# Layer 3, second half: normalising the output rows on ScalarE instead of VectorE

## The chip, the cores and the metric

The kernel runs on one core of one Trainium2 chip. The metric is device time in microseconds (us) for one execution of the whole program. The core's engines named here are PE (TensorE, matrix multiply), DVE (VectorE), ACT (ScalarE), POOL (GpSimd) and SP (SyncE, used here only to issue DMA transfers).

## The reference

Four graph-attention layers run one after the other over 3327 nodes of 256 features, all with the same adjacency matrix. Each is followed by a residual sum and a normalisation of every row. Only the last layer matters here; its cut form is:

```python
def _layernorm(x, axis=-1, eps=1e-5):
    m = jnp.mean(x, axis=axis, keepdims=True)
    v = jnp.var(x, axis=axis, keepdims=True)
    return (x - m) / jnp.sqrt(v + eps)

# layer 3: four heads of 64 features, two such passes one after the other
h = jnp.einsum('nf,hfd->hnd', x, W)
e = jax.nn.leaky_relu(f1[:, :, None] + f2[:, None, :], ALPHA)
e = jnp.where(adj[None, :, :] > 0, e, NEG)
att = jax.nn.softmax(e, axis=-1)
out = jax.nn.elu(jnp.einsum('hnm,hmd->hnd', att, h))

x = _layernorm(x + layer3(x, adj))      # the result
```

The change touches only the last line for layer 3: the last step of the normalisation, (x - mean) times 1/sqrt(var + eps), row by row.

## The kernel before

The nodes lie in 26 tiles of 128 rows (the last has 127). The tiles of the result are taken in four blocks of 7, 7, 6 and 6 tiles. The second pass of layer 3 is `many_heads(l3b, None, finish_last)`. For each block it loops over all 26 source tiles j:

- `adjacent` has SP load the adjacency tile `at` for (j, block) from DRAM (line 135 by way of `copy_rows`). There are three buffers for `at`, so SP issues the load of a step when DVE has finished with the tile of three steps earlier.
- `weigh` (line 1629) has DVE make four edge tiles `e`, one for each head, 128 x 896 elements in the blocks of seven and 128 x 768 (767) in the blocks of six. There are eight buffers for `e`, which is two steps of j.
- PE multiplies: line 1773 for the features and line 1781 for the row sums, both fp32. Within a step PE takes the first half of the block's columns for all four heads first, so it needs all four `e` tiles early in its step.

After a block's 26 steps its accumulators are copied out by ACT (lines 1800 and 1802), and `finish_last` for this block is put into the list `pending`. It is a generator: `work_off` takes one piece of it (up to a `yield`) in each step j of the **next** block. So the finishing of blocks 0, 1 and 2 runs among the steps of blocks 1, 2 and 3, and that of block 3 runs alone at the end. DVE, ACT and PE keep the order in which these pieces are emitted here; each engine works its instructions off in that order.

`finish_last` transposes the tiles back on PE (line 1923), scales and applies the elu on ACT and DVE (lines 1930 to 1950), takes the row statistics on DVE (lines 1952 and 1953) into `mv` (mean and variance of each tile), and then calls `scaled`:

```python
            nc.vector.tensor_scalar(rstd, mv[:, :, 1], EPS, None, op0=ALU.add)        # 250, DVE
            nc.gpsimd.tensor_tensor(rstd, rstd, minus_half..., op=ALU.pow)             # 251, POOL
            yield
            for s, it in enumerate(block):
                nc.vector.tensor_scalar(                                               # 257, DVE
                    h[it][:pn], ys[s][:pn], mv[:pn, s, 0:1], rstd[:pn, s : s + 1],
                    op0=ALU.subtract, op1=ALU.mult,
                )
                if s == len(block) // 2:
                    yield
            yield
```

In a block of seven, four tiles are normalised in one step of the loop and three in the following one. The finished tiles `h` are then written to `out_dram` by SP (line 135 again), one DMA for each tile. In SP's queue these writes stand among the loads of `at`.

Of the kernel before, what the change touches and what calls it, by code (L numbers as in the profile page):

```python
# [8 lines left out]
F32 = mybir.dt.float32  # L9
# [4 lines left out]
AF = mybir.ActivationFunctionType  # L14
ALU = mybir.AluOpType
# [4 lines left out]
P = 128  # L20
BANK = 512
SLOPE = 0.2
EPS = 1e-5
# [27 lines left out]
def gat_stack(  # L51
# [29 lines left out]
    nc = tc.nc  # L81
# [7 lines left out]
    def rows_of(it):  # L89
        return min(P, n - it * P)  # L90
# [4 lines left out]
    small = ctx.enter_context(tc.tile_pool(name="small", bufs=4))  # L95
# [4 lines left out]
    minus_half = const.tile([P, 1], F32, name="minus_half")  # L100
# [3 lines left out]
    h = [nodes.tile([P, dim], F32, name=f"h{it}") for it in range(nt)]  # L104
# [24 lines left out]
    def copy_rows(engine, dst, src):  # L129

        rows = dst.shape[0]
        whole = rows // 16 * 16
        for lo, hi in ((0, whole), (whole, rows)):
            if lo < hi:
                engine.dma_start(dst[lo:hi], src[lo:hi])
# [91 lines left out]
    blocks = [list(range(f, f + s)) for f, s in zip(firsts, sizes)]  # L227
# [20 lines left out]
    def scaled(block, ys, mv):  # L248
        rstd = small.tile([P, len(block)], F32, tag="rstds", name="rstds")
        nc.vector.tensor_scalar(rstd, mv[:, :, 1], EPS, None, op0=ALU.add)  # L250
        nc.gpsimd.tensor_tensor(  # L251
            rstd, rstd, minus_half.to_broadcast([P, len(block)]), op=ALU.pow
        )
        yield
        for s, it in enumerate(block):
            pn = rows_of(it)
            nc.vector.tensor_scalar(  # L257
# [6 lines that stand above are left out]
# [1242 lines left out]
    def layers(rs, early=0, rest=None):  # L1506
# [18 lines left out]
        def misc(banks):  # L1525
            spare[0] += 1
            i = banks[spare[0] % len(banks)]
            return ps.tile([P, BANK], F32, tag=f"b{i}", name="misc")
# [276 lines left out]
        def staged(units, stages):  # L1805

            last = max(at for _, at in units) + max(lag for lag, _ in stages)
            for step in range(last + 1):
                for lag, what in reversed(stages):
                    for unit, at in units:  # L1810
                        if at + lag == step:
                            what(unit)
                yield

        def inverses(block, sums, inv):

            full = [s for s, it in enumerate(block) if rows_of(it) == P]
            turned = misc((6, 7))
            for s, it in enumerate(block):
                pn = rows_of(it)  # L1820
                x, at0 = divmod(s, (len(block) + 1) // 2)
                nc.tensor.matmul(  # L1822
                    turned[:pn, s * heads : (s + 1) * heads],
                    sums[x][:, at0 * P : at0 * P + pn], heads_at, start=True, stop=True,
                )
            yield
            w = len(full) * heads
            nc.vector.reciprocal(inv[:, :w], turned[:, :w])
            if len(full) < len(block):
                pn = rows_of(block[-1])  # L1830
                nc.vector.reciprocal(inv[:pn, w : w + heads], turned[:pn, w : w + heads])
            yield
# [3 lines left out]
        def below(dst, v):  # L1836

            nc.scalar.activation(dst, v, AF.Relu, scale=-1.0)
            nc.scalar.activation(dst, dst, AF.Exp, scale=-1.0)
# [69 lines left out]
        def finish_last(b, o, sums):  # L1909
            block = blocks[b]  # L1910
            inv = small.tile([P, max(sizes) * heads], F32, tag="invs", name="invs", bufs=2)
            yield from inverses(block, sums, inv)
            mv = small.tile([P, len(block), 2], F32, tag="mvs", name="mvs")
            if rows_of(block[-1]) < P:
                nc.vector.memset(mv, 1.0)
            held = {}

            def back(s):
                it = block[s]
                pn = rows_of(it)  # L1920
                tp = misc((6, 7))
                for k in range(kc):
                    nc.tensor.transpose(
                        tp[:pn, k * P : (k + 1) * P], o[:, k, s * P : s * P + pn], ident
                    )
                both = work.tile([P, 2, 2 * P], F32, tag="spread", name="both", bufs=4)
                v, t = held[s] = both[:, 0, :], both[:, 1, :]
                if b < len(blocks) - 1:
                    for k in range(heads):
                        nc.scalar.activation(  # L1930
                            v[:pn, k * hd : (k + 1) * hd], tp[:pn, k * hd : (k + 1) * hd], AF.Copy,
                            scale=inv[:pn, s * heads + k : s * heads + k + 1],
                        )
                else:
                    nc.vector.tensor_tensor(
                        v[:pn].rearrange("p (h d) -> p h d", h=heads),
                        tp[:pn, :dim].rearrange("p (h d) -> p h d", h=heads),
                        inv[:pn, s * heads : (s + 1) * heads, None].to_broadcast([pn, heads, hd]),
                        op=ALU.mult,
                    )  # L1940
                below(t[:pn], v[:pn])

            def add(s):
                it = block[s]
                pn = rows_of(it)
                v, t = held.pop(s)
                nc.vector.scalar_tensor_tensor(  # L1947
                    v[:pn], t[:pn], -1.0, v[:pn], op0=ALU.add, op1=ALU.max
                )
                nc.vector.tensor_add(h[it][:pn], v[:pn], h[it][:pn])  # L1950
                stats = small.tile([P, nc.vector.BN_STATS_DIM], F32, tag="stats", name="stats")
                nc.vector.bn_stats(stats[:pn], h[it][:pn])  # L1952
                nc.vector.bn_aggr(mv[:pn, s, :], stats[:pn])

            yield from staged([(s, s) for s in range(len(block))], [(0, back), (3, add)])
            yield from scaled(block, [h[it] for it in block], mv)
            for it in block:
                pn = rows_of(it)
                copy_rows(nc.sync, out[it * P : it * P + pn, :], h[it][:pn])
            yield  # L1960
# [94 lines left out]
        l3b = Layer("l3b", "g", heads, True, load_heads(l3_w2, l3_a2), rate_d=rate3_d[1])  # L2055
        many_heads(l3a, l3b, finish_hidden)
        many_heads(l3b, None, finish_last)
        work_until(lambda: not pending)

# [80 lines left out]
```

## Time and profile before

| what | value |
|---|---|
| median of 3 runs | 2950.82 us (2949.16 to 2955.55) |
| the profiled execution, whole | 2953.03 us |
| its span, first to last instruction | 2951.3 us |
| mean granted TensorE clock over the span | 0.866 |
| PE busy in the span | 2329.5 us (79%) |
| DVE busy in the span | 2140.5 us (73%) |
| ACT busy in the span | 840.2 us (28%) |

All durations come from the one profiled execution, whose time is 1.7 us more than its span and 2.2 us above the median. The profile's times are counted from the start of the span. The second pass of layer 3 begins at about 2443 us. Its blocks 1, 2 and 3, among which `finish_last` runs, end their loops at about 2696, 2810 and 2922 us; the rest, to 2951, is the finishing of block 3. Shares over the whole span say little about this change: only about the last 360 us of the 2951 hold any of it.

### The profile page before, as it was taken

The page shows a single profiled execution, that of the slowest core. Times are in us where ns is not written, and L with a number is a line of the kernel's source. Part 1 is how long each engine was busy: PE and PEld are TensorE (multiplying, and loading weights), DVE is VectorE, ACT ScalarE, POOL GpSimd, SP SyncE. Part 2 cuts the span into 40 slices and gives each one's busy share as a digit, 9 for nine tenths or more (in the row PEclk, how much of TensorE's full clock was granted, in tenths as well). Part 3 has the DMA queues.
Part 4 walks back from the last instruction along what each step waited for, and adds up shares of the span by engine and source line. Part 5 has one row for each costly group of instructions (what it writes and reads, how often), then busy time and mean ns, then how long its engine had stood idle before and what let it go on. Part 6 is the DMA issues. An engine that isn't in the chain of part 4 may idle for free.

```text
span 2951.3 us, 45054 instructions
## 1 busy us (share of the span) xinstructions
PE 2329.5 (79%) x15841; PEld 1364.5 (46%) x15862; DVE 2140.5 (73%) x5634; ACT 840.2 (28%) x2358; POOL 991.6 (34%) x1061
## 2 busy tenths in 40 slices
PE   7466657556545416657899999999999999999997
PEld 4222323222222103325788888863556667534332
DVE  6789789968776527765445521138999999899997
ACT  3244445434334304543344311111010110110111
POOL 2676767777777777771000000000000000000000
PEclk8576777767776656889999999999999999999998
DMA  7685656445644444645776633331222222212211
GB/s 236 198 259 147 189 167 168 141 131 158 166 111 114 111 108 124 173 120 180 221 206 201 187 86 109 107 95 45 77 60 83 74 79 65 70 45 59 59 44 48
DMA packets 183854, 370.50 MB, mean 126 GB/s; under 512 B 35772, under 2 KB 124707, under 8 KB 182596
## 3 DMA queue, kind: packets, MB, share of 16 engines
q1 hardware_dynamic: 103994, 178.49, 21.2%
q0 software_dynamic: 51008, 155.70, 19.1%
q10 hardware_dynamic: 28618, 33.33, 3.3%
q8 instruction: 128, 2.10, 0.3%
q14 instruction: 106, 0.87, 0.1%
HBM read 327.52 MB, written 46.23 MB: 127 GB/s over the span
## 4 chain that ended last, share of the span: by engine, by line
PE 46%; DVE 5%; DMA 2%; issue 1%; ACT 0%; DVEq 0%; SPq 0%; ACTq 0%; POOL 0%; POOLq 0%
PE acc L1773 18%; PE acc L1723 16%; PE acc L1781 9%; DVE e L1629 3%; PE misc L1557 3%; DMA at<-at_d 1%; PE misc L1666 0%; DMA at_d<-at 0%; DMA at_i<-in_adj_t_dram 0%; DVE stats L1952 0%; DVE h L1950 0%; DVE h L1745 0%; DVE both L1947 0%; PE misc L1822 0%; DVE h L257 0%
## 5 line engine op out<-in xcount | busy, mean ns | idle before, releaser
L912 POOL DMA_INDIRECT g<-table_d,lst x894 | 850.8, 952 | 273.1 <-issue 243.4
L1629 DVE SCALAR_TENSOR_TENSOR e<-rate,feat,at 128x896 f32<-128x896 f32 (+4 forms) x832 | 843.4, 1080 | 58.6 <-PE acc L1781 47.2
L1015 PE MATMUL acc<-g,ident 128*128 128x512 f32 (+1 forms) x896 | 516.4, 721 | 257.3 <-ACT g L1012 232.5
L1773 PE MATMUL acc<-e,feat 128*32 128x384 f32 (+2 forms) x6656 | 697.4, 515 | 7.2 <-DVE h L1745 4.2
L1773 PEld LDWEIGHTS acc<-e,feat 128*32 128x32 f32 x6656 | 307.1, 110 | 305.3 <-issue 159.1
L1015 PEld LDWEIGHTS acc<-g,ident 128*128 128x128 f32 x896 | 199.2, 232 | 479.6 <-ACT g L1012 357.2
L1781 PE MATMUL acc<-e,feat 128*32 128x384 f32 (+3 forms) x3328 | 383.3, 512 | 0.0
L1012 ACT ACTIVATE g<-g,w 128x256 f32<-128x256 f32 x883 | 365.5, 495 | 0.4 <-ACT minus L489 0.4
L932 DVE TENSOR_TENSOR y<-g,minus_ps 128x1028 f32<-128x1028 f32 (+2 forms) x233 | 273.3, 1173 | 123.4 <-DMA g<-table_d,lst 113.6
L938 DVE SCALAR_TENSOR_TENSOR y<-y,a_ps 128x257 f32<-128x257 f32 x894 | 324.4, 418 | 26.5 <-PE a_ps L781 6.1
L1723 PE MATMUL acc<-feat,e 128*128 128x257 f32 (+2 forms) x1352 | 303.9, 382 | 7.4 <-DVE inv L1744 4.9
L251 POOL TENSOR_TENSOR rstds<-rstds,minus_half 128x7 f32<-128x7 f32 (+1 forms) x12 | 19.7, 1641 | 773.7 <-DVE rstds L250 773.7
L1723 PEld LDWEIGHTS acc<-feat,e 128*128 128x128 f32 (+2 forms) x1352 | 255.2, 191 | 45.3 <-issue 7.8
L1723 PE MATMUL acc<-feat,at 128*128 128x257 bf16 (+2 forms) x2028 | 237.8, 274 | 4.6 <-DMA at<-at_d 4.4
L1781 PEld LDWEIGHTS acc<-e,feat 128*32 128x32 f32 (+1 forms) x3328 | 162.1, 110 | 130.7 <-issue 88.1
L1723 PEld LDWEIGHTS <-at 128*128 128x128 bf16 (+2 forms) x2028 | 198.8, 99 | 38.3 <-DMA at<-at_d 4.9
L553 PE MATMUL v<-code,leads 65*128 65x512 bf16 (+1 forms) x182 | 83.3, 459 | 155.0 <-DVE cand L579 124.2
L1629 DVE SCALAR_TENSOR_TENSOR e<-rate,feat,at_i 128x896 f32<-128x896 f32 (+2 forms) x104 | 112.3, 1081 | 91.5 <-DMA at_i<-in_adj_t_dram 47.0
L579 DVE MAX8 cand<-v 128x8 f32<-128x104 f32 (+2 forms) x858 | 158.9, 260 | 21.6 <-PE v L556 21.3
L1609 POOL DMA_DIRECT2D rate3b_d<-rate_rows x4 | 2.1, 519 | 450.0 <-ACT rate_rows L1608 450.0
L1656 ACT CAST at<-at_i 128x896 bf16<-128x896 int32 (+2 forms) x104 | 92.0, 885 | 111.5 <-DMA at_i<-in_adj_t_dram 74.8
L553 PEld LDWEIGHTS <-leads 65*128 65x128 bf16 x182 | 22.3, 123 | 189.7 <-DVE cand L579 155.2
(248 smaller groups left out, 1829.3 us busy)
## 6 DMA issues: line engine op xcount, KB each, us to landing
adj_i<-in_adj_dram SPq DMA_DIRECT2D x75, 512.0 KB
at<-at_d SPq DMA_DIRECT2D x150, 224.0 KB
at_i<-in_adj_t_dram SPq DMA_DIRECT2D x50, 448.0 KB
at<-at_d SPq DMA_DIRECT2D x75, 192.0 KB
at<-at_d SPq DMA_DIRECT2D x75, 191.8 KB
g<-table_d,lst POOLq DMA_INDIRECT x894, 2.8
at_d<-at ACTq DMA_DIRECT2D x50, 224.0 KB
at_i<-in_adj_t_dram SPq DMA_DIRECT2D x25, 384.0 KB
```

The lines of the kernel that those rows point to most:

```text
L553: nc.tensor.matmul(v[:, :w], leads[:, b, :], code[:, :w], start=True, stop=False)
L579: nc.vector.max(spread[:, c0 + c, :], view(v[:, :w]))
L912: nc.gpsimd.indirect_dma_start(out=g[:, k - k0, :], out_offset=None, in_=table_d[:, :], in_offset=bass.IndirectOffsetOnAxis(ap=entry["lst" ...
L932: nc.vector.tensor_tensor(y, rows, minus_src[:, None, :].to_broadcast([P, m, dim + 1]), op=ALU.max)
L938: nc.vector.scalar_tensor_tensor(y, y, 1.0, a_ps[:, : dim + 1], op0=ALU.mult, op1=ALU.mult, accum_out=sc)
L1012: nc.scalar.activation(rows, rows, AF.Copy, scale=w[:, k : k + 1])
L1015: nc.tensor.matmul(dst, ident, rows, start=start, stop=stop)
L1629: nc.vector.scalar_tensor_tensor(e[:pn, : c1 - c0], self.rate[b][:pn, h_of, : c1 - c0], q, at[:pn, : c1 - c0], op0=ALU.max, op1=ALU.mult,)
L1656: nc.scalar.copy(at[:pn, :w], at_i[:pn, :w])
L1723: nc.tensor.matmul(accs[s][:pn, : dim + 1], a[:pj, s * P : s * P + pn], f[:pj, : dim + 1], start=(j == 0 and part == 0), stop=(j == nt - 1 ...
L1773: nc.tensor.matmul(accs[x][p][q : q + 32, : hi - lo], f[:pj, at0 : at0 + 32], es[at0 // hd][:pj, lo:hi], start=(j == 0), stop=(j == nt - 1),)
L1781: nc.tensor.matmul(accs[x][pairs][h_of * 32 : (h_of + 1) * 32, : hi - lo], f[:pj, dim + h_of : dim + h_of + 1].to_broadcast([pj, 32]), es[ ...
```

## The change

`finish_last` no longer calls `scaled`. It makes the same `rstd` (DVE add, POOL power), then one further small DVE instruction makes `shift` = -mean * rstd for all tiles of the block. The tiles are then normalised by ACT as `h * rstd + shift`, both taken as one value for each row. In the last block every second tile (s = 1, 3, 5) is still normalised by DVE with the old instruction. The places of the `yield`s stay.

```diff
-            yield from scaled(block, [h[it] for it in block], mv)
+            rstd = small.tile([P, len(block)], F32, tag="rstds", name="rstds")
+            shift = small.tile([P, len(block)], F32, tag="rstds", name="shifts")
+            nc.vector.tensor_scalar(rstd, mv[:, :, 1], EPS, None, op0=ALU.add)
+            nc.gpsimd.tensor_tensor(
+                rstd, rstd, minus_half.to_broadcast([P, len(block)]), op=ALU.pow
+            )
+            yield
+            nc.vector.scalar_tensor_tensor(
+                shift, mv[:, :, 0], -1.0, rstd, op0=ALU.mult, op1=ALU.mult
+            )
+            for s, it in enumerate(block):
+                pn = rows_of(it)
+                if b == len(blocks) - 1 and s % 2:
+                    nc.vector.tensor_scalar(
+                        h[it][:pn], h[it][:pn], mv[:pn, s, 0:1], rstd[:pn, s : s + 1],
+                        op0=ALU.subtract, op1=ALU.mult,
+                    )
+                else:
+                    nc.scalar.activation(
+                        h[it][:pn], h[it][:pn], AF.Identity,
+                        bias=shift[:pn, s : s + 1], scale=rstd[:pn, s : s + 1],
+                    )
+                if s == len(block) // 2:
+                    yield
+            yield
             for it in block:
                 pn = rows_of(it)
                 copy_rows(nc.sync, out[it * P : it * P + pn, :], h[it][:pn])
```

The instruction orders of the two kernels, engine by engine, differ in these places only:

- DVE loses 20 instructions of line 257 in blocks 0, 1 and 2 (7, 7 and 6) and 3 of 6 in block 3; it gains one `shift` in each block, in the place where the first of line 257 stood.
- ACT gains 7, 7, 6 and 3 activations, behind the last elu activation of the same block and ahead of the next block's copies of line 1800.
- SP had, in blocks 0 to 2, four writes of `out_dram`, one load of `at`, and the other two or three writes. Now all six or seven writes stand together behind the twentieth (in the last such place the nineteenth) load of the block, and the load that stood between them comes after. In block 3 the first two writes are exchanged: tile 94 before tile 93.
- PE and POOL keep their order.

## Prediction

> **What bounds the kernel now.** I read three things in this order: the chain of work that ended last, the busy time of the engines in two neighbouring stretches, and the timelines of DVE and PE where the removed instructions stand.
>
> The chain, on the page, says who sets the time over the whole span:
>
> ```profile
> span 2951.3 us, 45054 instructions
> ...
> PE 46%; DVE 5%; DMA 2%; issue 1%; ACT 0%; DVEq 0%; SPq 0%; ACTq 0%; POOL 0%; POOLq 0%
> ```
>
> PE leads, DVE is a small second. The question is whether the DVE part holds the removed instructions. The busy time in two stretches of block 2 of the second pass (the columns are stretch, length, busy time and number for PE, weight loads, DVE, ACT and POOL, then clock, DMA share, GB/s):
>
> ```profile
> 2730.00:2784.00 54.00, 53.28 (x562) 19.41 (x566) 53.28 (x81) 10.57 (x36) 2.11 (x1) 1.00 0.20 58
> 2784.00:2843.00 59.00, 59.00 (x719) 24.24 (x712) 55.83 (x62) 4.64 (x12) 0.00 (x0) 1.00 0.19 52
> ```
>
> PE looks full in both. But it ends 719 matmuls in 59 us (12.2 per us) in the second stretch and 562 in 54 us (10.4 per us) in the first, at the same clock of 1.00. In the first PE is waiting inside its own records, and DVE is the engine without a gap. `finish_last` of block 1 runs in the first stretch only. ACT is busy a fifth of it. The timeline of DVE there (start, duration, line, tiles, number):
>
> ```profile
> 2765.92 3.79 DVE L1629 SCALAR_TENSOR_TENSOR e<-rate,feat,at 128x768 f32<-128x768 f32 x4
> 2769.63 0.16 DVE L250 TENSOR_SCALAR rstds<-mvs 128x7 f32<-128x7 f32 x1
> 2769.70 3.80 DVE L1629 SCALAR_TENSOR_TENSOR e<-rate,feat,at 128x768 f32<-128x768 f32 x4
> 2773.42 1.38 DVE L257 TENSOR_SCALAR h<-h,mvs,rstds 128x256 f32<-128x256 f32 x4
> 2774.71 3.80 DVE L1629 SCALAR_TENSOR_TENSOR e<-rate,feat,at 128x768 f32<-128x768 f32 x4
> 2778.43 1.05 DVE L257 TENSOR_SCALAR h<-h,mvs,rstds 128x256 f32<-128x256 f32 x3
> 2779.40 1.01 DVE L1629 SCALAR_TENSOR_TENSOR e<-rate,feat,at 128x768 f32<-128x768 f32 x1
> ```
>
> Start to start, four edge tiles take 3.72 us, the four tiles of line 257 1.29 us and the three 0.97 us. The timeline of PE, only the first group of each of three steps:
>
> ```profile
> 2772.70 2.74 PE L1773 MATMUL acc<-e,feat 128*32 128x384 f32 x28
> ...
> 2776.57 3.80 PE L1773 MATMUL acc<-e,feat 128*32 128x384 f32 x28
> ...
> 2781.51 3.56 PE L1773 MATMUL acc<-e,feat 128*32 128x384 f32 x28
> ```
>
> 2.74 us is the group undisturbed; 3.80 and 3.56 us hold waits for edge tiles that came late. From start to start a free step takes 3.87 us (2772.70 to 2776.57), the two others 4.94 and 4.69 us (the next group starts at 2786.20). Last, the tail, and ACT's idle time behind block 1's elu:
>
> ```profile
> 2938.70 1.32 POOL L251 TENSOR_TENSOR rstds<-rstds,minus_half 128x6 f32<-128x6 f32 x1 [58.73 <-DVE rstds L250]
> 2940.05 2.03 DVE L257 TENSOR_SCALAR h<-h,mvs,rstds 128x256 f32<-128x256 f32 x6 [1.50 <-POOL rstds L251]
> 2940.49 3.65 SPq L135 DMA_DIRECT2D out_dram<-h  x7
> ```
>
> ```profile
> 2810.59 0.48 ACT L1800 COPY o<-acc 128x384 f32<-128x384 f32 x1 [55.90 <-PE acc L1773]
> ```
>
> **What the Trainium skill says.** "Perfetto Trace Analysis", section Tensor Engine Instruction, states that the end of a matmul in a profile is estimated and not observed. Here that is why I count PE's starts and not its busy time: 53.28 us busy of 54 hides about a seventh of lost pace. "VectorE: DVE Perf Modes", the section on the perf-mode tier table, puts fp32 tensor_scalar between SBUF tiles at twice the rate of tensor_tensor. The trace agrees in direction: 0.32 us from start to start for line 257, 0.46 us for the 256-element addition of line 1950 (2764.90 to the following record at 2765.36). So the removed instructions are the cheap kind. "ScalarE: Activation LUTs" says under Table sets that identity lies in every set beside exp, so the new activations load no table; the built order of ACT shows no load there either.
>
> **The change part by part.**
>
> *Blocks 0 to 2: what goes.* DVE loses 7, 7 and 6 instructions of line 257. What that is worth is the time PE lost to them, read from its starts:
> - block 1's loop (finishing block 0): starts 2653.41, 2657.92, 2663.28, 2668.49, 2673.01. Free steps are 4.51 us, the two late ones 5.36 and 5.21: 0.85 + 0.70 = 1.55 us.
> - block 2's loop (finishing block 1): 4.94 and 4.69 against 3.87: 1.07 + 0.82 = 1.89 us.
> - block 3's loop (finishing block 2): starts 2884.64, 2889.57, 2893.93, so 4.93 and 4.36 against 3.87: 1.06 + 0.49 = 1.55 us.
>
> The sum is 4.99 us, less than the 6.5 us that the 20 instructions take of DVE (2.26 + 2.26 + 1.95 from start to start): while the delay lasts, PE uses up the little it was ahead, and afterwards DVE at 3.72 us a step is faster than PE at 3.87. *What is late next:* PE itself. After the change DVE needs 3.72 + 0.07 us in the step with `shift`, under 3.87; in block 1's loop 4.24 + 0.07 against 4.51. So the whole 4.99 us should go, and no more.
>
> *What DVE gains.* One `shift` over 6 or 7 values, of the kind of line 250 (0.16 us long, 0.07 us from start to start). It waits for POOL's power, as the first of line 257 did. In the loops the power has ended by then (2769.94 + 2.11 = 2772.05, against 2773.42), so it waits for nothing. Behind it in DVE's queue stand edge tiles, so if that cover of 1.4 us went, each microsecond would cost one. Cost taken: 0, since the step stays below PE's.
>
> *What ACT gains.* The trace of before has no activation with both scale and bias as a value per row. The nearest row, line 1838 with 256 elements and neither, takes 0.42 us; that is the lower end. The price in "ScalarE: Activation LUTs" gives an estimate of 280 + 93 + 0.833 x 256 = 586 ns, 0.49 us from start to start. I take 0.49: seven tiles are 3.5 us. ACT has 55.90 us of idle time after that point in block 2's loop, and what stands behind the activations in its queue is line 1800 at the loop's end, so the cost is 0. If ACT took a full microsecond each it would still be idle in time; only SP would notice.
>
> *SP's queue.* The six or seven writes now stand together, each waiting for its ACT instruction, and the following load of `at` stands behind them. From `shift` at time t the last write goes out at about t + 3.6 (ACT) + 0.45 (one issue; 1.44 us for three), so t + 4.1. The load becomes due when DVE frees the buffer, at t + 3.8. It is some 0.3 us late. It is used two steps of at least 3.72 us later, 7.4 us after the due time. How long such a load takes to land is not in the trace. A POOL-issued row load of 1536 KB landed in 7.0 us, so 192 KB takes less; "DMA: Bandwidth & Descriptors", section Anatomy of one DMA, has 2.0 us and bytes over 436 GB/s, fitted for the POOL path, which gives an estimate of 2.5 us. Late load and landing come to 2.8 to 7.3 us of 7.4: cost 0, but at the upper end with nothing to spare.
>
> *Tail.* Before, the first row tile was ready at 2940.05 + 0.42, and SP issued seven writes in 3.65 us from 2940.49, slower than DVE made the tiles (2.03 us for six). So issue sets the end, and halving the arithmetic gains nothing. After, `shift` goes first; tile 94 on DVE starts about 0.1 us later, and SP asks for it first. ACT's tile 93 is there at about 2940.25 + 0.59 = 2940.84, before SP is free again at about 2941.1. Cost 0.10 us; bounds 0 and 0.4 (SP waiting for ACT twice).
>
> *Sum.* 4.99 - 0.10 = 4.89 us less. The profiled execution of 2953.03 us would become 2948.1 and its span 2946.4; the median of 2950.82 becomes 2945.9, 0.17% less. 0.2% of this kernel (5.9 us, a time of 2944.9) is about what a measurement of it can tell from no change, and the forecast lies just 1.0 us short of that.
>
> **The rivals.**
>
> *The relief is larger (about 2944).* All of DVE's 6.5 us and a little more would count if PE's lead carried over from stretch to stretch, say because a fuller lead at the end of one block spares part of the next wait at line 1947. For it: DVE has no gap from 2730 to 2784. Against: between the two waiting stretches DVE waits for PE again (2.20 us at 2823.09), so the lead was full anyway. 2950.8 - 6.5 = 2944.3.
>
> *The relief is hidden (about 2950.9).* PE's waits could come from elsewhere, from the transposes of line 1923 or from loads. Then only the 0.1 us of the tail is left. Against: the long groups stand exactly in the two steps behind line 257, in all three blocks.
>
> *Slower: SP's queue holds back `at` (2957 and more).* The place is the load behind the seven writes. If one ACT tile takes x, the load is late by 7x - 3.3 us, and with a landing of 7.0 us DVE starves for 7x - 3.7 us in each of three places; PE follows, since it has no lead there. At x = 0.49 that is nothing. It outweighs the gain from 1.6 us a place, x = 0.76, and reaches 0.2% slower at 3.6 us a place, x = 1.04, twice the estimate: 2950.8 - 4.9 + 10.8 = 2956.7. A write that waits for an earlier write's completion would do the same. For it: the writes did stand in two groups before. Against: before, four writes in a row took 2.84 us and were followed by a load with no wait on DVE's side.
>
> **How the numbers follow.** The main case has 76%. It runs from a gain of 2.5 us (a third of the waits stays) to 8 us, about 2943 to 2948.5: the three runs of before scatter over 6.4 us, so the median itself can be off by 2. Its middle lies so near the 0.2% line that I split it, 42 beyond and 34 within. Larger relief has 8%, hidden relief 5%, slower 11%. Faster by over 0.2% is 42 + 8 = 50%; within 34 + 5 = 39%; slower 11%. The range for 8 in 10 is 2942 to 2950.5: it takes in the main case and the larger relief and most of the hidden case, and leaves out SP's.
>
> **What would show it.** In the changed profile the groups of 28 matmuls behind `shift` should take 2.74 us and the steps 3.87 (4.51 in block 1's loop), with none of 3.80. DVE should pass from edge tiles to `shift` to edge tiles. ACT's new instructions should last 0.5 to 0.6 us. The first write of the tail should start about 0.1 us later after the power's end. I am wrong on the gain if the long groups stay, and wrong on SP if DVE's edge tiles show a wait for the DMA of `at` in those steps.

## The result, and the profile after

| what | before | after |
|---|---|---|
| median of 9 runs | 2957.91 us (2949.16 to 2961.46) | 2950.14 us (2944.41 to 2952.86) |
| ratio, after to before | | 0.9977, 95% interval 0.9967 to 0.9987 |
| profiled execution: whole, span | 2953.03, 2951.3 us | 2952.55, 2950.7 us |

By the ratio the change takes 6.8 us off (3.9 to 9.8), where 0.17% (4.9 us) was forecast; the two medians alone differ by 7.8. The nine runs of before hold the three that were known (2949.16 to 2955.55) and six later ones, all between 2957.54 and 2961.46.

The two profiled executions differ by only 0.6 us in span. To see what that hides, one needs two marks that both kernels have. The reciprocals of line 1828 open the finishing of a block; they come once in each block's loop. Timeline of DVE, before (start, duration, line, tiles):

```profile
2590.72 0.33 DVE L1828 RECIPROCAL invs<-misc 128x28 f32<-128x28 f32 x1
2717.39 0.32 DVE L1828 RECIPROCAL invs<-misc 128x28 f32<-128x28 f32 x1
2830.68 0.30 DVE L1828 RECIPROCAL invs<-misc 128x24 f32<-128x24 f32 x1
2926.81 0.28 DVE L1828 RECIPROCAL invs<-misc 128x20 f32<-128x20 f32 x1 [5.97 <-PE misc L1822]
```

The same after:

```profile
2595.15 0.32 DVE L1828 RECIPROCAL invs<-misc 128x28 f32<-128x28 f32 x1
2720.26 0.33 DVE L1828 RECIPROCAL invs<-misc 128x28 f32<-128x28 f32 x1
2831.66 0.30 DVE L1828 RECIPROCAL invs<-misc 128x24 f32<-128x24 f32 x1
2926.21 0.28 DVE L1828 RECIPROCAL invs<-misc 128x20 f32<-128x20 f32 x1 [5.97 <-PE misc L1822]
```

From mark to mark, before: 126.67, 113.29 and 96.13 us. After: 125.11, 111.40 and 94.55, which is 1.56, 1.89 and 1.58 us less. The sum, 336.09 to 331.06 us, is a gain of 5.03 us; it is called *the loops* below. From the last mark to the end of the span, *the tail*, it is 24.49 us in both (the span is printed to 0.1 us, so a tail is good to 0.05). And the first mark, which the change doesn't touch, came 4.43 us later in this one execution. That is why the spans look alike.

The chain on the page of after: against before DVE went from 5 to 4% and issue from 1 to 0%; PE's share is the same.

```profile
span 2950.7 us, 45073 instructions
...
PE 46%; DVE 4%; DMA 2%; issue 0%; ACT 0%; SPq 0%; DVEq 0%; POOL 0%; POOLq 0%; ACTq 0%
```

The place of the gain, in block 2's loop. Timeline of DVE, after:

```profile
2768.79 3.79 DVE L1629 SCALAR_TENSOR_TENSOR e<-rate,feat,at 128x768 f32<-128x768 f32 x4
2772.49 0.17 DVE L1958 TENSOR_SCALAR rstds<-mvs 128x7 f32<-128x7 f32 x1
2772.57 3.81 DVE L1629 SCALAR_TENSOR_TENSOR e<-rate,feat,at 128x768 f32<-128x768 f32 x4
2776.28 0.17 DVE L1963 SCALAR_TENSOR_TENSOR shifts<-mvs,rstds 128x7 f32<-128x7 f32 x1
2776.36 14.04 DVE L1629 SCALAR_TENSOR_TENSOR e<-rate,feat,at 128x768 f32<-128x768 f32 x15
```

Where four and three instructions of line 257 stood there is one `shift` of 0.08 us from start to start, and edge tiles on both sides. Timeline of PE, after, the first group of each step:

```profile
2770.40 4.05 PE L1773 MATMUL acc<-e,feat 128*32 128x384 f32 x28
...
2775.57 2.74 PE L1773 MATMUL acc<-e,feat 128*32 128x384 f32 x28
...
2779.45 2.74 PE L1773 MATMUL acc<-e,feat 128*32 128x384 f32 x28
...
2783.32 2.74 PE L1773 MATMUL acc<-e,feat 128*32 128x384 f32 x28
```

The groups of 3.80 and 3.56 us are gone and the steps are 3.87 us (2775.57, 2779.45, 2783.32). In block 3's loop the same groups take 2.73 us; in block 1's the undisturbed group is one of 24 matmuls and 2.53 us, and its steps are 4.51 us. The group of 4.05 us ahead of them stayed; it belongs to the steps with the elu and the statistics. Before had it too:

```profile
2767.53 4.04 PE L1773 MATMUL acc<-e,feat 128*32 128x384 f32 x28
```

ACT and SP in the same place, timelines of after:

```profile
2776.49 3.55 ACT L1974 ACTIVATE h<-h,shifts,rstds 128x256 f32<-128x256 f32 x7 [18.91 <-DVE shifts L1963]
```

```profile
2777.11 3.76 SPq L135 DMA_DIRECT2D out_dram<-h  x7
2780.96 6.99 SPq L135 DMA_DIRECT2D at<-at_d  x3
```

Seven activations in 3.55 us, after 18.91 us of idle time. The load of `at` behind the seven writes goes out at 2780.96. DVE's edge tiles run on without a wait, so nobody missed it. In none of the three loops of after does DVE wait for a load of `at`: apart from 0.25 us in block 1's that the profile calls "issue" (no cause shows), it waits there for PE only.

The tail, timeline of after:

```profile
2938.13 1.32 POOL L1959 TENSOR_TENSOR rstds<-rstds,minus_half 128x6 f32<-128x6 f32 x1 [57.19 <-DVE rstds L1958]
2939.48 0.17 DVE L1963 SCALAR_TENSOR_TENSOR shifts<-mvs,rstds 128x6 f32<-128x6 f32 x1 [1.52 <-POOL rstds L1959]
2939.56 1.05 DVE L1969 TENSOR_SCALAR h<-h,mvs,rstds 128x256 f32<-128x256 f32 x3
2939.68 1.58 ACT L1974 ACTIVATE h<-h,shifts,rstds 128x256 f32<-128x256 f32 x3 [5.39 <-DVE shifts L1963]
2940.00 3.57 SPq L135 DMA_DIRECT2D out_dram<-h  x7
```

SP's first write is that of DVE's first tile (s = 1, the forecast's tile 94; its tile 93 is s = 0, on ACT). The arithmetic is shared between two engines, DVE's part takes 1.05 us instead of 2.03 and ACT's 1.58, SP's issue takes 3.57 us instead of 3.65, and the end comes 11.25 us after the power's end (2939.45 to 2950.7), against 11.28 before (2940.02 to 2951.3). So the time that was saved on the arithmetic doesn't reach the end. What does is in the instructions that close the program. Those at the line of the `with` around the kernel, in the last 16 us of after (number, shortest/median/longest in ns, first to last start):

```profile
L2120 POOLq DRAIN  x3: 46/103/7831, 2942.0 to 2950.4; - x3
L2120 SPq DRAIN  x3: 7/7/13, 2947.7 to 2950.1; - x3
```

POOL's queue has a DRAIN of 7831 ns from 2942.0, so to 2949.8. Ahead of it stands one more instruction, of the line of the final `tc.If`:

```profile
L2102 POOLq INC_SWDGE_SEM  x1: 2081/2081/2081, 2939.9 to 2939.9; - x1
```

Power to 2939.45, this one from 2939.9, the drain from 2942.0 to 2949.8, the end at 2950.7: a chain on POOL. SP reaches its first DRAIN at 2947.7, 4.1 us after the issue of its last write and 2.1 us ahead of the end of POOL's drain. Before shows the same order, with POOL's drain over at 2950.4:

```profile
L2096 POOLq DRAIN  x3: 46/103/7831, 2942.6 to 2951.0; - x3
L2096 SPq DRAIN  x3: 7/7/13, 2948.2 to 2950.7; - x3
```

The view of the chain that ended last doesn't show this: after, it ends at ACT's last activation.

### The profile page after: what moved, and what is told of

The parts are those of the page before. It is cut to its first block, busy times and chain, and to the rows that moved or that the text cites. A ratio compares the mean times of both kernels' runs of the same rounds, so it can differ in the third digit from the quotient of the medians.

```text
span 2950.7 us, 45073 instructions
## 1 busy us (share of the span) xinstructions
PE 2317.0 (79%) x15862; PEld 1359.2 (46%) x15862; DVE 2134.7 (72%) x5615; ACT 852.4 (29%) x2381; POOL 992.3 (34%) x1061
## 4 chain that ended last, share of the span: by engine, by line
PE 46%; DVE 4%; DMA 2%; issue 0%; ACT 0%; SPq 0%; DVEq 0%; POOL 0%; POOLq 0%; ACTq 0%
PE acc L1773 18%; PE acc L1723 16%; PE acc L1781 9%; DVE e L1629 3%; PE misc L1557 3%; DMA at<-at_d 1%; PE misc L1666 0%; DMA at_d<-at 0%; DMA at_i<-in_adj_t_dram 0%; DVE stats L1952 0%; DVE h L1950 0%; DVE h L1745 0%; DVE both L1947 0%; PE misc L1822 0%; DMA dst<-in_l_att_dram 0%
## 5 line engine op out<-in xcount | busy, mean ns | idle before, releaser
L1015 PE MATMUL acc<-g,ident 128*128 128x512 f32 (+1 forms) x896 | 505.5, 708 | 262.3 <-ACT g L1012 246.1
```

The lines of the kernel that those rows point to most:

```text
L1015: nc.tensor.matmul(dst, ident, rows, start=start, stop=stop)
```

## The experiments

All times in us. *Loops* and *tail* are read from each run's trace as above. e1 to e4 ran on a chip on which the whole takes about 3400: its part before the loops is some 440 longer (in the changed kernel POOL's last gather, line 912, starts at 1739.4 there and at 1342.6 here, so 397 of it have passed by then). Loops and tail are the same there. A dash stands where only one execution was measured; its loops and tail can be compared, its whole time can't.

| run | before the loops | loops | tail | ratio to before, 95% interval |
|---|---|---|---|---|
| before | 2590.72 | 336.09 | 24.49 | |
| after | 2595.15 | 331.06 | 24.49 | 0.9977 (0.9967 to 0.9987) |
| e1_after_again | 3034.72 | 331.05 | 24.43 | 0.9990 (0.9977 to 1.0004) |
| e2_before_again | 3038.31 | 336.05 | 24.44 | 1.0001 (0.9984 to 1.0019) |
| e3_loops_only | 3035.30 | 331.04 | 24.46 | 0.9976 (0.9961 to 0.9990) |
| e4_tail_only | 3028.48 | 336.05 | 24.47 | 1.0003 (0.9989 to 1.0017) |
| e5_no_norm | 2591.83 | 331.08 | 24.49 | - |
| e6_norm_twice | 2597.43 | 345.06 | 24.41 | - |
| e7_add_on_pool | 2593.90 | 328.71 | 24.79 | 0.9975 (0.9968 to 0.9982) |
| e8_tail_all_act | 2591.38 | 331.08 | 24.44 | - |
| e9_tail_two_queues | 2599.54 | 331.06 | 24.50 | - |
| e11_power_on_dve | 2590.32 | 331.03 | 23.15 | - |
| e12_spread | 2597.67 | 327.48 | 24.45 | - |
| e13_both | 2599.80 | 327.48 | 23.32 | 0.9967 (0.9956 to 0.9977) |

**Where the gain is, and what a ratio can tell** (e1 to e4). e1 and e2 are the two kernels unchanged. e3 keeps the old norm in the last block, e4 in all others:

```diff
+            if b == len(blocks) - 1:          # e3; in e4: if b < len(blocks) - 1
+                yield from scaled(block, [h[it] for it in block], mv)
+            else:
                 rstd = small.tile([P, len(block)], F32, tag="rstds", name="rstds")
...
```

> The changed kernel once more. I use two measures of its profile: the loops, from the first reciprocal of line 1828 to the one of the last block (336.1 us in the profile of before, 331.1 in that of after), and the tail, from there to the end (24.5 in both). Relief theory (the loops give 5.0 us, nothing else differs): loops 331.1, tail 24.5, and over the rounds a ratio of 0.9983. Rival (the change also gains some 2 us before the loops): ratio 0.9977 or below, and the time before the loops shorter than that of before in most profiles.

> The kernel before against itself, to see what a ratio is worth when nothing differs. Relief theory, with scatter from the part before the loops: ratio within 0.999 to 1.001, loops 336.1 and tail 24.5 as in its other profile, while the time before the loops differs by several us. Rival (the time before the loops is a property of the kernel): that time repeats within 1 us of 2590.7.

> Blocks 0 to 2 as changed, the last block normalised by VectorE alone as before. Relief theory: all of the gain, loops 331.1 us, tail 24.5, ratio 0.9983 as for the whole change. Rival (the alternation in the tail carries part of the gain): ratio near 0.9995.

> Only the last block as changed; blocks 0 to 2 normalised by VectorE as before. Relief theory: loops 336.1 us, tail 24.5 (the issue of the seven writes sets its end), ratio 1.000. Rival (the tail gains from two engines): tail 1 us shorter or more, ratio 0.9995 or below.

Measured: the loops of e3 are those of after (331.04), the tail of e4 is that of before (24.47). So all 5 us come from blocks 0 to 2 and nothing from the last block, in the traces. e1's rival, a further gain before the loops, isn't borne out: its ratio is 0.9990 and not 0.9977 or below, and on that chip the part before the loops took 3034.72 and 3035.30 us with the changed loops, 3038.31 and 3028.48 with the old ones. The last two, e2 and e4, have the same code up to the last block and differ by 9.8 us: that part doesn't repeat. The ratios say it less sharply. Before against itself, 14 runs against 59, has an interval of 0.18% to each side: that is as large as the effect. e1's and e4's intervals contain 1, e3's and after's do not, and those of e1, e3 and after all contain 5.0 us of their time (0.9985 of 3400, 0.9983 of 2951).

**Whether ACT or SP take anything back** (e5). The norm is left out in blocks 0 to 2. ACT then has no new work there, and SP's writes wait for the residual addition only: in the trace they go out one in a step among the loads of `at`, and not six or seven together:

```diff
-                if b == len(blocks) - 1 and s % 2:
+                if b < len(blocks) - 1:
+                    pass
+                elif s % 2:
```

> The changed kernel without the normalising instructions of blocks 0 to 2 (their rows are written out unscaled; mean, power and shift are still made). Relief theory (after the change PE alone sets the pace of those steps, and ACT's instructions and SP's grouped writes cost nothing): loops 331.05 us as with them, within 0.1. Rival (ACT or SP holds something back): loops shorter by 0.3 us or more, and a first group of PE that lasts over 2.74 us in the changed kernel's steps behind shift.

Measured: 331.08, against 331.06 with the norm on ACT. So neither the 20 activations nor the grouped writes cost anything in the loops.

**Whether DVE's time there goes to the end one for one** (e6), on the kernel before: each instruction of line 257 of blocks 0 to 2 is made once more, into a scratch tile.

```diff
+                if b < len(blocks) - 1:
+                    again = work.tile([P, dim + 1], F32, tag="v", name="again")
+                    nc.vector.tensor_scalar(again[:pn, :dim], h[it][:pn], ...)
                 nc.vector.tensor_scalar(h[it][:pn], h[it][:pn], ...)
```

> The kernel before, with each instruction of line 257 in blocks 0 to 2 issued once more into a scratch tile. Relief theory: where the wait stands already, each further microsecond of DVE goes to the end, so the 20 copies add 1.29 + 0.97 us in two blocks and 1.30 + 0.65 in the third: loops 336.07 + 6.47 = 342.5 us. So the first 6.5 us cost 5.0 and the second 6.5. Rival (PE's waits come from elsewhere): loops near 336.1.

Measured: loops 8.97 us longer instead of 6.5. The miss is in the price of the copy, not in the path. Timeline of DVE in e6:

```profile
2783.27 0.41 DVE L1966 TENSOR_SCALAR again<-h,mvs,rstds 128x256 f32<-128x256 f32 x1
2783.72 0.41 DVE L1970 TENSOR_SCALAR h<-h,mvs,rstds 128x256 f32<-128x256 f32 x1
2784.04 0.41 DVE L1966 TENSOR_SCALAR again<-h,mvs,rstds 128x256 f32<-128x256 f32 x1
2784.49 0.41 DVE L1970 TENSOR_SCALAR h<-h,mvs,rstds 128x256 f32<-128x256 f32 x1
```

The instruction that overwrites `h` starts 0.45 us after the copy that reads it; the next copy follows after 0.32, the overlap that line 257 had before. Four pairs take 3.09 us instead of 1.29 (2783.27 to 2786.36), three 2.31 instead of 0.97: 1.80 + 1.34 us more in blocks of seven, twice, and 2.69 in the block of six, in all 8.97. DVE's added time arrives whole. In the change 6.5 us of it went and 5.03 arrived: PE's own pace is reached before all is used.

**More of DVE's finishing taken away** (e7): the residual addition of blocks 0 to 2 goes to POOL, and the statistics move to the step after it.

```diff
-                nc.vector.tensor_add(h[it][:pn], v[:pn], h[it][:pn])
+                if b == len(blocks) - 1:
+                    nc.vector.tensor_add(h[it][:pn], v[:pn], h[it][:pn])
+                    take(s)
+                else:
+                    nc.gpsimd.tensor_tensor(h[it][:pn], v[:pn], h[it][:pn], op=ALU.add)
...
+            stages = [(0, back), (3, add)] + ([(4, take)] if b < len(blocks) - 1 else [])
+            yield from staged([(s, s) for s in range(len(block))], stages)
```

> The changed kernel, with the residual addition of line 1950 in blocks 0 to 2 moved to POOL, and the statistics taken one step later so that DVE does not wait for POOL. Relief theory: DVE still binds in those steps (5.18 us against 3.87), so each of 20 additions is worth its 0.46 us, 9.1 us in all, less what PE's own pace takes back at the end of the stretch, some 0.5 us for each block: loops about 323.5 us, ratio against the kernel before 0.9957. Rival (POOL and DVE share a path to memory, so DVE's edge tiles get slower while POOL adds): edge tiles of over 1.0 us in those steps, loops above 327.

Measured: 328.71, so 2.35 us less than after and not 7.5. Timelines of DVE and POOL in e7:

```profile
2749.69 4.28 DVE L1629 SCALAR_TENSOR_TENSOR e<-rate,feat,at 128x768 f32<-128x768 f32 x4
2749.92 1.38 POOL L1954 TENSOR_TENSOR h<-both,h 128x256 f32<-128x256 f32 x1 [3.69 <-DVE both L1947]
```

```profile
2734.46 0.73 POOL L1954 TENSOR_TENSOR h<-both,h 128x256 f32<-128x256 f32 x1 [75.69 <-DVE both L1947]
```

Four edge tiles take 4.28 us where POOL adds beside them and 3.79 elsewhere; the addition takes 1.38 us there, and 0.73 where it started in a wait of DVE, as the first of this loop did. So the rival came true: DVE gives back 0.49 us for each addition that it was spared. A step with a row tile takes it 5.06 us (2739.57 to 2744.63, in block 2's loop) in place of 5.18, and little of the saving is left. The tail is 0.3 us longer than in after; why stays open. "SBUF — State Buffer" of the Trainium skill, section SBUF: two separate sides, states that DVE instructions with two SBUF inputs and POOL instructions share one pair of ports, an exclusive lock held for a whole instruction. These numbers agree in direction with that, on both sides of it; no run here shows the lock itself.

**What sets the tail's end** (e8, e9, e11). e8 has ACT normalise all six tiles of the last block; e9 has ACT's queue issue the last two tiles' writes; e11 takes the last block's power from POOL and makes it with 11 small instructions on DVE:

```diff
-                if b == len(blocks) - 1 and s % 2:          # e8
+                if False:
...
-                copy_rows(nc.sync, out[it * P : it * P + pn, :], h[it][:pn])          # e9
+                queue = nc.scalar if b == len(blocks) - 1 and it >= block[-2] else nc.sync
+                copy_rows(queue, out[it * P : it * P + pn, :], h[it][:pn])
...
+            else:          # e11: b is the last block
+                nc.vector.tensor_scalar(y_i, rstd.bitcast(I32), 1, None, op0=ALU.logical_shift_right)
+                nc.vector.tensor_scalar(y_i, y_i, -1.0, float(0x5F3759DF), op0=ALU.mult, op1=ALU.add)
+                for _ in range(3):
+                    nc.vector.tensor_tensor(sq, y, y, op=ALU.mult)
+                    nc.vector.scalar_tensor_tensor(sq, sq, -0.5, rstd, op0=ALU.mult, op1=ALU.mult)
+                    nc.vector.scalar_tensor_tensor(y, sq, 1.5, y, op0=ALU.add, op1=ALU.mult)
...
```

> The changed kernel with all six tiles of the last block on ScalarE. Relief theory (the issue of the writes sets the tail): six tiles at 0.49 us from start to start keep just ahead of SP's 0.51 us a write, so only the later first tile counts: tail 24.45 + 0.25 = 24.7 us, loops 331.05. Rival (the pace of normalising sets the tail, and the alternation is what keeps it short): tail 25.5 us or more.

> The changed kernel, with the writes of the last block's last two row tiles issued by ScalarE's queue and not by SyncE's. Time from the last block's reciprocals to the end of the span (24.49 us after the change). If the issue of the seven writes sets the end: some 1 us shorter, 23.5 us. If the end hangs on GpSimd (its power, then its own closing drain of 7.8 us): unchanged, 24.4 to 24.5 us. If ScalarE's issue stands behind its activations and costs more than SyncE's: longer, 24.7 us or more.

> The changed kernel, with the power of the last block alone computed on VectorE (a first guess from the exponent bits, then three Newton steps: 11 small instructions), so that GpSimd has nothing to do in the tail. 11 small dependent instructions at 0.1 to 0.2 us in place of 1.53 us between the end of line 1958 and the start of shift: the row tiles become ready 0.4 us earlier to 0.7 us later. If the issue of the writes sets the end, the tail follows that: 24.1 to 25.2 us against 24.49. If GpSimd's closing drain, which starts behind its last instruction, sets the end: the drain starts earlier, no longer stands last, and the tail is shorter by 1 to 2.5 us, 22.0 to 23.5 us, however late the row tiles are by these 0.7 us.

Measured in e8: SP's seven writes take 4.66 us, 1.09 longer, and the tail is 24.44. In e9 SP issues four in 2.06 us and ACT three in 1.35, done 0.9 us earlier after the first (2944.38 to 2947.02), and the tail is 24.50. The writes of e8, then of e9:

```profile
2936.55 4.66 SPq L135 DMA_DIRECT2D out_dram<-h  x7
```

```profile
2944.38 2.06 SPq L135 DMA_DIRECT2D out_dram<-h  x4
2945.67 1.35 ACTq L135 DMA_DIRECT2D out_dram<-h  x3
```

Longer or shorter issue, the end stays: POOL's drain is over at 2946.1 in e8 and 2954.2 in e9, SP at its first DRAIN at 2945.2 and 2951.1. In e11 `shift` starts 2.42 us after line 1958 does (2932.91 to 2935.33), in after 1.70 us, so the row tiles come 0.72 us later, and yet the tail is 1.34 us *shorter*. Closing instructions of e11:

```profile
L2136 POOLq DRAIN  x3: 46/103/7831, 2932.6 to 2944.2; - x3
L2136 SPq DRAIN  x3: 7/7/13, 2943.6 to 2943.9; - x3
```

POOL's long drain now starts at 2932.6, before DVE has made `rstd` (2932.91), and is over at 2940.4. SP comes last, to its first DRAIN at 2943.6. In after it was the other way round (2949.8 and 2947.7). So before and after the change the tail ended with POOL's chain of power and drain; with the power gone, SP ends it. In all 14 traces SP reaches that DRAIN 4.0 to 4.4 us after the last of the writes has been issued, in e9 too, where ACT issued it (2947.02 to 2951.1). That SP waits there for the writes to land fits this, but it is inferred.

**What is left in the loops** (e12): in blocks 0 to 2 the row tiles of the finishing start in every second step.

```diff
-            yield from staged([(s, s) for s in range(len(block))], [(0, back), (3, add)])
+            apart = 1 if b == len(blocks) - 1 else 2
+            yield from staged([(s, apart * s) for s in range(len(block))], [(0, back), (3, add)])
```

> The changed kernel, with the seven row tiles of the finishing of blocks 0 to 2 started in every second step and not in every step, so that VectorE's 1.9 us of work on each lie beside twice as many edge steps. Time of the three loops (331.06 us after the change). A step of edge tiles takes VectorE 3.72 us and TensorE 3.87, so each of the 6 or 7 further steps can take up 0.15 us: about 1 us a block, 328 us in all, if VectorE's excess over TensorE in these steps is what is left. If TensorE alone sets the pace already: 331.0. If the later statistics push the norm and its writes into the next block, or the transposes then stand in TensorE's way at worse places: 332 or more.

Measured: 327.48, 3.58 us less than after: 1.91, 0.92 and 0.75 us by block. Timeline of DVE in e12, two starts of the elu with eight edge tiles between them:

```profile
2745.75 0.41 DVE L1947 SCALAR_TENSOR_TENSOR both<-both 128x256 f32<-128x256 f32 x1
...
2747.22 7.51 DVE L1629 SCALAR_TENSOR_TENSOR e<-rate,feat,at 128x768 f32<-128x768 f32 x8
2754.64 0.42 DVE L1947 SCALAR_TENSOR_TENSOR both<-both 128x256 f32<-128x256 f32 x1
```

Two neighbouring starts in after:

```profile
2756.96 0.42 DVE L1947 SCALAR_TENSOR_TENSOR both<-both 128x256 f32<-128x256 f32 x1
...
2762.14 0.42 DVE L1947 SCALAR_TENSOR_TENSOR both<-both 128x256 f32<-128x256 f32 x1
```

In e12 two steps take DVE 8.89 us. In after such a step takes 5.18 us and a following one of PE's 3.87, in all 9.05: 0.16 us less. Between seven tiles lie six added steps, between six tiles five: 0.96 and 0.80 us, where 0.92 and 0.75 were measured. In block 1's loop a step is 4.24 us on DVE and 4.51 on PE, so an added step takes up 0.27, six of them 1.6 of the 1.91 measured. Most of the rest may be the 0.25 us of "issue" that DVE's row shows in after's loop and not in e12's. The expectation had used 0.15 throughout.

**Both together** (e13: the edits of e11 and e12).

> The changed kernel with two more edits together: the finishing of blocks 0 to 2 spread over every second step, and the last block's power on VectorE. If the two gains are of separate places, they add: loops 327.5 us (as with the spreading alone), tail 23.15 us (as with the power alone), so 4.9 us less than the changed kernel and 10.0 us less than the kernel before, a ratio of 0.9966 to it. If the spreading only moves the wait into the tail, the tail is longer than 23.2 us and the ratio about 0.998.

Measured: loops 327.48, tail 23.32, ratio to before 0.9967 (0.9956 to 0.9977), medians 2946.47 and 2957.41. The two gains add. Against the kernel before, this version takes 9.8 us less by the ratio and 9.8 by loops and tail (8.61 + 1.17); against the changed kernel it is 4.75 us less by loops and tail, while the two ratios have intervals that overlap.

## Why the prediction was right, and where it was wrong

- *The gain in the loops* was right, block by block. Forecast 1.55, 1.89 and 1.55 us, measured 1.56, 1.89 and 1.58; e3 shows that it stands without the tail. Reading PE's starts, and not its busy time, gave it. Three of the rivals fall with it: not all 6.5 us of DVE arrived, the waits were not from elsewhere, and no load of `at` came late.
- *"What is late next: PE itself"* held for the steps behind `shift` (3.87 us, no group above 2.74). It was too broad for the loop: e7 and e12 take another 2.35 and 3.58 us out by touching the steps of the elu and the statistics, where the group of 4.05 us had stayed. The forecast said that long groups stand exactly in the two steps behind line 257; the trace of before also had the one of 4.04 us at 2767.53, ahead of them.
- *ACT's price* was right: 0.58 us for one and (3.55 - 0.58) / 6 = 0.49 us from start to start. "ScalarE: Activation LUTs" of the Trainium skill, section What ACT_TABLE_LOAD costs, has the constants behind the estimate of 586 ns; the 23 activations have a median of 585 ns.
- *The cheap kind.* The forecast compared 0.32 us for line 257 with 0.46 for the addition of line 1950. These are not alike: the 0.46 runs to an instruction that needs the sum, the 0.32 to one that needs nothing from it. By their own durations in the trace of before the two take 0.41 and 0.42 us, so at this size no factor of two shows. The forecast's sum doesn't use it.
- *SP's queue* was right in its effect, cost 0 (DVE has no wait for `at`, and e5). Its size was off: the load behind the writes went out 4.68 us after `shift` (2776.28 to 2780.96) and not 4.1, since ACT began 0.2 us after `shift` did and SP took 0.54 us for each write where ACT needed 0.49 for a tile. That is about 0.9 us after its due time and not 0.3. With the landing of 7.0 us that the forecast allowed for, its own sum would give a wait of 0.5 us in each place. None shows, so the load took less than that, some 6.5 us at most.
- *The tail* was wrong in its mechanism: "So issue sets the end" fails by e8 and e9. POOL's chain of power, 2.08 us and a drain of 7.83 us sets it. The cost was 0.00 in place of 0.10, because the power stands ahead of everything that the change altered. The first write did start 0.08 us later after the power's end (0.55 against 0.47), as forecast, but SP had 2.1 us to spare. The forecast saw the writes in the timeline and didn't ask what follows them; the closing instructions were in the trace of before.
- *The sum and its place.* This is the step that failed: the forecast took 0.2% (5.9 us) for what a measurement can tell from no change, and so put its 4.89 us, 0.17%, on the side of no difference, if by 1.0 us only. Nine runs against nine had an interval of 0.10% to each side (2.9 us), and their 0.23% is clear of zero. The sum itself was hardly off: with the tail at 0 instead of -0.10 it is 5.03 us, which lies within the 3.9 to 9.8 of the whole runs. Whether the 1.8 us between 5.03 and 6.8 are more than scatter isn't shown; in the traces nothing but the loops differs in a way that repeats, and the first mark moves from 2590 to 2600 us over the traces of this kind and from 3028 to 3038 on the other chip. There the interval of e1, 22 runs against 59, did not clear zero, so it was not certain that the whole runs would tell. The other term that was mis-sized is "the median itself can be off by 2": with six more runs before's median went from 2950.82 to 2957.91, by 7.1 us. After came out at 2950.14 where 2945.9 was forecast. That this still lies in the range of 2942 to 2950.5 is in part luck, since the range is only 8.5 us wide. One figure of the range was misnamed: a gain of 2.5 us is half of the 4.99, so half of the waits would stay and not a third.
- *How good one comparison is.* The ratios of e1, e3, after, e7 and e13 (3.4, 8.2, 6.8, 7.4 and 9.8 us) against loops and tail (5.0, 5.0, 5.0, 7.1 and 9.8) show it: each agrees within its interval, none is good to 1 us in its own right. What makes the part before the loops vary was not tried.

## What to carry to other kernels

Where two engines run in lockstep through a few buffers, a record of "busy" on the follower hides its waits: take the starts of a repeating group, find the undisturbed step, and sum what the others take beyond it; that sum was right to 0.04 us here. Do it for every step of the loop and not only for those that the change touches. To check a change of a few microseconds in thousands, measure between marks that both traces have, since the rest of the program can move by more than the effect. And before a tail is costed, follow every engine's queue to the last instruction: the one that closes the program may wait for an engine that the chain of waits doesn't name.

## What the runs showed of the hardware

- POOL's queue closes with the instruction INC_SWDGE_SEM of 2.08 us and a DRAIN of 7831 ns to the nanosecond, in all 14 traces here, also where POOL's last work lies before the tail (e11, e13). Nothing in these runs shows what it drains.
- A DVE tensor_scalar of 128x256 fp32 that overwrites the tile which the instruction before it reads starts 0.45 us after it; after one that reads another tile the same form follows in 0.32 us (e6). Whether the overwriting or the shared input makes the difference was not separated.
- Side by side, a POOL addition of 128x256 fp32 costs DVE's four edge instructions of 128x768 together 0.49 us, and they make the addition 0.65 us longer (e7: 3.79 to 4.28 and 0.73 to 1.38).
- Small DVE instructions of six elements that each need the one before take 0.20 us from start to start (e11: 2933.12 to 2935.13 for ten steps); where the next instruction doesn't need the result it starts after 0.08 (after: 2776.28 to 2776.36).
